# Windowed attention with a gated output: the first four query tiles take their exponentials with the queries on the partitions

## The chip, the cores and the metric

The kernel runs on one core of one Trainium2 chip. The metric is the time of one execution on the device in microseconds (us), as the median of several runs. A profile is one such execution with the hardware profiler on. Its page and its trace name the engines: PE is TensorE's matmuls and PEld its weight loads, DVE is VectorE, ACT is ScalarE, POOL is GpSimd, and SP is the engine whose queue issues nearly all transfers here.

## What is computed

The input x has 8 batches of 1024 tokens with 512 features. In short:

```
xn     = layernorm(x)                          # no weights
q,k,v  = xn @ Wq.T + bq, xn @ Wk.T + bk, xn @ Wv.T + bv     # 16 heads of 32
scores = q @ k.T / sqrt(32), where (i % 256) >= (j % 256), else -1e30
attn   = softmax(scores) @ v
s      = attn @ Wo.T + bo
g      = silu(clip((xn @ sign(fw).T) * scale + bias, -100, 100))
out    = x + s * g                             # all float32
```

A query i sees key j when i modulo 256 is not below j modulo 256. The kernel reorders the tokens so that the four tokens with the same place in a window stand side by side. In that order the mask is block causal: query tile i (128 tokens) sees key tiles 0 to i, and only the tile on the diagonal needs a mask inside it.

## The kernel before

**Tiling.** A batch has 8 token tiles of 128, which form two halves: query tiles 0 to 3 (called f=0) and 4 to 7 (f=1). The 16 heads form 4 groups of 4, and one group fills the 128 partitions of q and k. So there are 32 pairs (b, g) of a batch and a group of heads. Each pair goes through 9 steps, n = 0 to 8, written out in the loop at L1109.

**Two passes over the scores.** Softmax needs a maximum over the keys for each query. The first pass (`maxima_quad`, L501) computes scores with the queries on the partitions into one PSUM tile of four banks, the "quad", one bank for each head, and VectorE reduces it to maxima (`pm`, L537). `shift_parts` (L542) splits the maxima into three bf16 parts, and `shift_rows` (L561) turns these into rows with TensorE. The second pass (`probs_quad`, L586) computes the scores again, now with the keys on the partitions. It first subtracts the maxima by a matmul of the rows with minus ones (L592), then adds the scores (L603) and the mask (L614). ScalarE takes the exponential of all four banks in one instruction (L627), and the result has the layout that `attend_quad` (L633) needs to multiply by v (L640). `S_QUADS` (L43) says which query tiles and key columns are in the first pass's quad of each step, and `T_QUADS` (L56) does so for the second pass.

**Sums.** The denominators are sums over the keys, which lie on the partitions. GpSimd adds up the probability tiles of a half (`add_probs`, L649), and TensorE adds over the partitions with a matmul by ones (`sum_keys`, L678). VectorE inverts the sum in four pieces (`invert`, L713) and multiplies (`normalise_heads`, L717). In the last pair, `sum_quad` (L693) sums each quad on TensorE instead.

**Order of the work.** There is room for one quad alone (`ps_q` has one buffer). The two passes alternate in it: the second pass of pair (b, g) and the first pass of the next pair. While ScalarE or VectorE empties the quad, TensorE does other work: the attend of the step before, and pieces from a list of "beside" work (`Beside.fill`, L953): q and k projections (`q20` is group 2, half 0), values (`V`), gate (`G`, `H`), output (`O`), layernorm turns (`N`). The strings `STEADY`, `OPENING` and `CLOSING` (L804) write that list out by hand for each pair, with a due place for each transfer. Every piece has a cost in us by the program's own count (0.86 for a chunk of four matmuls over 512 columns), and each step is given a share. Engines take their instructions in program order. All transfers but four are issued by SP, in program order too.

**Storage.** Wq and Wk stay transposed in SBUF for the whole run (`wT`, L244). Probability tiles have two buffers (`probs`), the running totals one each for f=0 and f=1.

## Time and profile before

| what | value |
|---|---|
| median of 3 runs | 2209.55 us (2209.39 to 2209.75) |
| the profiled execution's own time | 2209.57 us |
| its span in the trace | 2207.8 us |
| PE busy | 2177.1 us, 99% |
| POOL busy | 1325.8 us, 60% |
| DVE busy | 1276.7 us, 58% |
| ACT busy | 876.8 us, 40% |
| DMA | 93.60 MB, mean 42 GB/s |
| granted TensorE clock | 1.00 in every stretch |
| first and last exponential (L627) start | 79.9 and 2171.7 us |

The span is the time from the first to the last recorded instruction; the rest of the execution's time lies around it. Busy times of PE come from modelled ends of pipelined matmuls, so that neighbours overlap. What a piece of work costs TensorE is better read from a timeline, as the distance from its start to the start of the next piece. The 288 exponentials are 9 for each of 32 pairs.

### The profile page before, as it was taken

Reading aid. Unit: us, or ns where it says so; the run is one execution under the profiler, and the core shown is the slowest. Engines: PE = TensorE matmul, PEld = TensorE weight load, DVE = VectorE, ACT = ScalarE, POOL = GpSimd, SP = SyncE. Lnnn points to the kernel's source line nnn. Section 1 sums busy time; section 2 is a strip of 40 time slices with the busy share of each in tenths; the row PEclk is TensorE's granted clock in tenths of the full one; section 3 lists DMA queues with packets and bytes.
Section 4 is the critical chain, followed back from the end, with each engine's and each line's share of the span. In section 5 each row is a group of like instructions: output and inputs, shape, how many; then the busy total and the mean of one; then the engine's idle time right before and its main releaser. Section 6 shows DMA issues by size and latency. Waiting matters only on the chain. (4 is left out here: it accounts for less than half of the span.)

```text
span 2207.8 us, 57362 instructions
## 1 busy us (share of the span) xinstructions
PE 2177.1 (99%) x26015; PEld 865.2 (39%) x26015; DVE 1276.7 (58%) x1635; ACT 876.8 (40%) x862; POOL 1325.8 (60%) x1198
## 2 busy tenths in 40 slices
PE   8999999999999999999999999999999999999998
PEld 4334433334333443333443333334333443333333
DVE  4556556665557655566555665565655665555564
ACT  2235433444344444344343443434443343333332
POOL 1256566666566656576557765556765666755562
PEclk9999999999999999999999999999999999999999
DMA  4001000121001210012000120002100111000113
GB/s 167 2 16 34 12 7 30 54 73 35 25 25 40 73 35 25 25 57 75 16 25 25 63 68 16 25 26 68 63 16 26 45 58 64 11 21 25 45 54 125
DMA packets 49676, 93.60 MB, mean 42 GB/s; under 512 B 5388, under 2 KB 5656, under 8 KB 49432
## 3 DMA queue, kind: packets, MB, share of 16 engines
q1 hardware_dynamic: 48728, 88.76, 12.1%
q8 instruction: 203, 3.33, 0.6%
q10 hardware_dynamic: 704, 1.18, 0.2%
q14 instruction: 41, 0.34, 0.0%
HBM read 56.37 MB, written 33.55 MB: 41 GB/s over the span
## 5 line engine op out<-in xcount | busy, mean ns | idle before, releaser
L659 POOL TENSOR_TENSOR p<-p,p 128x512 f32<-128x512 f32 x930 | 1096.6, 1209 | 390.0 <-ACT p L627 238.8
L537 DVE TENSOR_REDUCE pm<-s 128x4 f32<-128x2048 f32 (+3 forms) x384 | 664.0, 1750 | 583.6 <-PE s L525 581.7
L627 ACT ACTIVATE p<-t 128x2048 f32<-128x2048 f32 x288 | 540.8, 1878 | 830.7 <-PE t L614 434.7
L715 DVE RECIPROCAL aT<-aT 128x128 f32<-128x128 f32 x256 | 230.3, 928 | 214.6 <-ACT aT L676 214.6
L525 PE MATMUL s<-k,q 32*128 32x512 f32 (+3 forms) x3072 | 315.3, 504 | 1.1 <-ACT q L401 0.8
L640 PE MATMUL av<-p,v 128*32 128x512 f32 (+3 forms) x3072 | 307.4, 495 | 1.6 <-DVE aT L719 1.4
L603 PE MATMUL t<-q,k 32*128 32x512 f32 (+3 forms) x3072 | 301.2, 486 | 0.0
L358 PE MATMUL k_ps<-xnT,wkT 128*32 128x512 f32 (+3 forms) x2832 | 254.9, 477 | 1.7 <-ACT wkT L274 0.7
L358 PE MATMUL q_ps<-xnT,wqT 128*32 128x512 f32 (+2 forms) x2656 | 254.1, 497 | 1.7 <-ACT shift L572 0.8
L358 PE MATMUL v_ps<-wvT,xnT 128*32 128x512 f32 (+3 forms) x2728 | 254.8, 489 | 0.0
L358 PE MATMUL o_ps<-woT,aT 128*32 128x320 f32 (+2 forms) x2568 | 243.9, 503 | 1.5 <-ACT shift L572 0.8
L741 POOL TENSOR_TENSOR s<-s,xb 128x512 f32<-128x512 f32 x63 | 86.2, 1369 | 211.8 <-DVE s L740 209.7
L603 PEld LDWEIGHTS t<-q,k 32*128 32x128 f32 x3072 | 145.1, 185 | 23.4
L358 PEld LDWEIGHTS k_ps<-xnT,wkT 128*32 128x32 f32 x2832 | 83.7, 110 | 169.0 <-issue 138.3
L358 PEld LDWEIGHTS q_ps<-xnT,wqT 128*32 128x32 f32 x2656 | 79.0, 110 | 174.0 <-issue 151.3
L358 PEld LDWEIGHTS v_ps<-wvT,xnT 128*32 128x32 f32 x2728 | 79.2, 109 | 168.6 <-issue 143.4
L525 PEld LDWEIGHTS s<-k,q 32*128 32x128 f32 x3072 | 117.0, 185 | 52.0 <-ACT p L627 42.2
L456 PE MATMUL y_ps<-fwT,x 128*128 128x512 f32 x464 | 135.4, 418 | 1.7 <-ACT k L401 1.3
L640 PEld LDWEIGHTS av<-p,v 128*32 128x32 f32 x3072 | 70.3, 108 | 169.4 <-issue 134.7
L358 PEld LDWEIGHTS o_ps<-woT,aT 128*32 128x32 f32 x2568 | 76.1, 110 | 151.4 <-issue 133.1
L429 POOL TENSOR_TENSOR x<-xnT,x 128x512 fp32r<-128x512 f32 x58 | 74.2, 1279 | 99.9 <-ACT x L428 99.9
L435 POOL TENSOR_SCALAR y<-y 128x512 f32<-128x512 f32 x64 | 39.6, 618 | 152.9 <-DVE y L434 101.1
(96 smaller groups left out, 1478.1 us busy)
## 6 DMA issues: line engine op xcount, KB each, us to landing
g<-t SPq DMA_DIRECT2D x64, 256.0 KB, 2.0
gb<-g SPq DMA_DIRECT2D x64, 256.0 KB, 2.8
xb<-in_L_attn_x_dram SPq DMA_DIRECT2D x64, 256.0 KB, 3.1
out_dram<-s SPq DMA_DIRECT2D x63, 256.0 KB, 2.5
x<-in_L_attn_x_dram SPq DMA_DIRECT2D x62, 256.0 KB, 3.1
wq_st<-in_L_attn_Wq_dram SPq DMA_DIRECT2D x2, 512.0 KB, 5.1
wv_st<-in_L_attn_Wv_dram SPq DMA_DIRECT2D x2, 512.0 KB
fw_st<-in_L_ffn_weights_dram SPq DMA_DIRECT2D x2, 512.0 KB, 9.5
```

What stands on the lines that cost most here:

```text
L358: nc.tensor.matmul(hold[0][cols, lo:hi], lhsT=lhsT[:, cols], rhs=rhs[:, lo:hi], start=(i == 0 and lo == 0), stop=(i == n - 1), skip_group_ ...
L429: nc.gpsimd.tensor_tensor(part[1], src, part[0].bitcast(F32), ALU.subtract)
L435: nc.gpsimd.tensor_scalar(y[0], y[0], MAX_VAL, -MAX_VAL, ALU.min, ALU.max)
L456: nc.tensor.matmul(hold[0], lhsT=part[i][:, c, :], rhs=wT["fw"][:, c, :], start=(i == 0 and c == 0), stop=(i == 1 and c == NC - 1),)
L525: nc.tensor.matmul(sc[:, h, at : at + w], lhsT=qt[b, g][head_rows(h), i * P : (i + 1) * P], rhs=kt[b, g][head_rows(h), lo:hi], start=(at = ...
L537: nc.vector.tensor_reduce(pm[:, 0 if lo == 0 else 1, i, :], sc[:, :, at : at + w], AX.X, ALU.max)
L603: nc.tensor.matmul(sc[:, h, at : at + w], lhsT=kt[b, g][head_rows(h), j * P : (j + 1) * P], rhs=qt[b, g][head_rows(h), q0 : q0 + w], start ...
L627: nc.scalar.activation(pt[:, :, :width], sc[:, :, :width], AF.Exp, scale=SCALE)
L640: nc.tensor.matmul(av[b, g, f][head_rows(h), lo : lo + w], lhsT=vt[b, j][:, g * P + h * DK : g * P + (h + 1) * DK], rhs=pts[b, g, n][:, h, ...
L659: nc.gpsimd.tensor_tensor(t[:, hs, lo : lo + w], t[:, hs, lo : lo + w], p[:, hs, at : at + w], ALU.add)
L715: nc.vector.reciprocal(r, r)
L741: nc.gpsimd.tensor_tensor(s, s, xr, ALU.add)
```

## The change

The eight query tiles are now treated in two ways.

- **Tiles 0 to 3** ("direct"): the first pass's quad is exponentiated where it stands, with queries on the partitions. VectorE's reductions of these tiles run for two heads at a time and give the negated maxima (`nm`). ScalarE takes the exponential for each tile and head with that as a bias, and collects the sum along the row (`own_probs`). VectorE inverts the sums, and GpSimd multiplies the probabilities by them (`own_scale`). VectorE turns every 32x32 block (`own_turn`), and 16 transfers from SBUF to SBUF, each of 32 partitions, put the blocks where a full transpose has them (`move`). `own_attend` multiplies by v. There is no second pass, no row of maxima, no total and no sum by TensorE for these tiles.
- **Tiles 4 to 7** keep the second pass. Their quads are 7 in place of 9.

The steps 0, 3 and 6 hold direct quads, and the steps 0 and 3 have no quad of the second pass. Turns are issued at the head of steps 1, 4 and 8, the moves four at a time at each call of `fill`, and the attends come in steps 4, 7 and the next pair's 1. To make room in SBUF, the transposed Wq and Wk are written to DRAM once and fetched by group (two transfers of 256 KB for each pair). 1/sqrt(32) goes into q. The beside lists, the shares of the steps and the due places of the transfers are written anew. In the last pair the outputs of tiles 0 to 3 (`P`) are beside work, where all eight came after it. The core of the diff:

```diff
 S_QUADS = [
+    [(3, 0, 512)],
+    [(7, 0, 512)],
+    [(6, 0, 512)],
+    [(2, 0, 384), (0, 0, 128)],
     [(4, 0, 512)],
     [(5, 0, 512)],
-    [(6, 0, 512)],
-    [(7, 0, 512)],
+    [(1, 0, 256), (5, 512, 768)],
     [(7, 512, 1024)],
-    [(4, 512, 640), (6, 512, 896)],
-    [(5, 512, 768), (1, 0, 256)],
-    [(3, 0, 512)],
-    [(0, 0, 128), (2, 0, 384)],
+    [(6, 512, 896), (4, 512, 640)],
 ]
...
 T_QUADS = [
-    [(1, 0, 0)],
-    [(1, 1, 0)],
-    [(1, 2, 0)],
-    [(1, 3, 0)],
-    [(1, 4, 0)],
-    [(1, 5, 128), (1, 7, 384)],
-    [(1, 6, 256), (0, 2, 256)],
-    [(0, 0, 0)],
-    [(0, 1, 128), (0, 3, 384)],
+    [],
+    [(0, 0)],
+    [(1, 0)],
+    [],
+    [(2, 0)],
+    [(3, 0)],
+    [(6, 256)],
+    [(5, 128), (7, 384)],
+    [(4, 0)],
 ]
 NQ = len(T_QUADS)
 assert NQ == len(S_QUADS)
-FIRST = {1: 0, 0: 6}
-LAST = {1: 6, 0: 8}
-TOTAL = {1: 0, 0: 7}
+FIRST, LAST = 1, 8
+DIRECT = {0: 4, 3: 4, 6: 2}
...
+    swapped = pool("swapped", 1)
...
+    def keep_weight(name):
+        wd[name] = kept_w.tile([NC, P, NC, P], F32, tag=name, name=f"{name}_d")
+        for c in range(NC):
+            nc.sync.dma_start(
+                wd[name].rearrange("g p c e -> c p g e")[c],
+                wT[name][c].rearrange("p (g e) -> p g e", g=NC),
+            )
+
+    def fetch_slice(name, b, g):
+        t = slices.tile([P, NC, P], F32, tag=name, name=f"{name}_{b}_{g}")
+        nc.sync.dma_start(t, wd[name][g])
+        wslice[name, b, g] = t
...
-                bias=bias[:, g : g + 1], scale=1.0,
+                bias=bias[:, g : g + 1], scale=SCALE if which == "q" else 1.0,
...
+        own = [seg for seg in placed(n) if seg[0] < 4]
+        if own:
+            nm = small.tile([P, 2, NH], F32, tag="nm", name=f"nm_{b}_{g}_{n}", bufs=2)
+            direct[b, g, n] = {"sc": sc, "nm": nm, "own": own}
+            for h in range(0, NH, 2):
+                for k, (i, lo, hi, at) in enumerate(own):
+                    nc.vector.tensor_reduce(
+                        nm[:, k, h : h + 2], sc[:, h : h + 2, at : at + hi - lo],
+                        AX.X, ALU.max, negate=True,
+                    )
+        for i, lo, hi, at in placed(n):
+            if i >= 4:
+                nc.vector.tensor_reduce(
+                    pm[:, 0 if lo == 0 else 1, i - 4, :], sc[:, :, at : at + hi - lo],
+                    AX.X, ALU.max,
+                )
+    def own_probs(b, g, n):
+        it = direct[b, g, n]
+        it["p"] = probs.tile([P, NH, HALF], F32, tag="p", name=f"pd_{b}_{g}_{n}").rearrange(
+            "p h t -> p (h t)"
+        )
+        ls = it["sum"] = small.tile([P, 2, NH], F32, tag="ls", name=f"ls_{b}_{g}_{n}", bufs=2)
+        view = by_slot(it["p"], n)
+        for h in range(NH):
+            for k, (i, lo, hi, at) in enumerate(it["own"]):
+                nc.scalar.activation(
+                    view[:, h, at // P : (at + hi - lo) // P],
+                    it["sc"][:, h, at : at + hi - lo].rearrange(
+                        "p (k r t) -> p k r t", r=NH, t=MT
+                    ),
+                    AF.Exp, bias=it["nm"][:, k, h : h + 1], scale=1.0,
+                    accum_out=ls[:, k, h : h + 1],
+                )
+
+    def own_scale(b, g, n):
+        it = direct[b, g, n]
+        view = by_slot(it["p"], n)
+        used = it["sum"][:, 0 : len(it["own"]), :]
+        nc.vector.reciprocal(used, used)
+        for h in range(NH):
+            for k, (i, lo, hi, at) in enumerate(it["own"]):
+                part = view[:, h, at // P : (at + hi - lo) // P]
+                nc.gpsimd.tensor_scalar(part, part, it["sum"][:, k, h : h + 1], None, ALU.mult)
+    def own_turn(b, g, n):
+        it = direct[b, g, n]
+        size = NH * DIRECT[n] * P
+        t = swapped.tile([P, NH * HALF], F32, tag="pt", name=f"pt_{b}_{g}_{n}")
+        move_some(len(moves))
+        nc.vector.transpose(t[:, 0:size], it["p"][:, 0:size])
+        block = size // NH
+
+        def move(q, r):
+            if "x" not in it:
+                it["x"] = swapped.tile([P, NH * HALF], F32, tag="px", name=f"px_{b}_{g}_{n}")
+            nc.sync.dma_start(
+                it["x"][r * MT : (r + 1) * MT, q * block : (q + 1) * block],
+                t[q * MT : (q + 1) * MT, r * block : (r + 1) * block],
             )
+
+        moves.extend(lambda q=q, r=r: move(q, r) for r in range(NH) for q in range(NH))
...
+    def own_attend(b, g, n):
+        it = direct.pop((b, g, n))
+        k = DIRECT[n]
+        x = it["x"][:, 0 : NH * k * P].rearrange("p (q h k t) -> p h k q t", q=NH, h=NH, k=k, t=MT)
+        first = (b, g, 0) not in av
+        if first:
+            av[b, g, 0] = ps_a.tile([P, HALF], F32, tag="av", name=f"av_{b}_{g}_0")
+        for i, lo, hi, at in it["own"]:
+            for j in range(lo // P, hi // P):
+                for h in range(NH):
+                    nc.tensor.matmul(
+                        av[b, g, 0][head_rows(h), i * P : (i + 1) * P].rearrange(
+                            "p (q t) -> p q t", t=MT
+                        ),
+                        lhsT=vt[b, j][:, g * P + h * DK : g * P + (h + 1) * DK],
+                        rhs=x[:, h, at // P + j - lo // P],
+                        start=first,
+                        stop=(j == hi // P - 1),
+                        skip_group_check=True,
+                    )
+                first = False
+        if n == 6:
+            copy_heads(b, g, 0)
...
+            sides[b, g] = Beside(beside(b, g), [1.8, 1.43, 1.86, 0.86, 1.86, 1.86, 1.36, 2.3, 1.86])
...
+            move_some(4)
...
+        if nxt and n in (1, 4, 8):
+            own_turn(*nxt, {1: 0, 4: 3, 8: 6}[n])
+        spent = 0.0
+        if n in (0, 3):
+            if nxt:
+                maxima_quad(*nxt, n)
             if n == 0:
+                shift_rows(b, g)
+            if before:
+                attend_quad(*before)
+            if nxt:
+                own_probs(*nxt, n)
+            if n == 0 and old:
+                copy_heads(*old, 1)
+                spent += fill(1.2, turns=0)
+                sum_keys(*old)
+            spent += fill(share - spent - 1.0 if nxt else share - spent)
+            if nxt:
+                own_scale(*nxt, n)
+        else:
+            probs_quad(b, g, n)
+            if before:
+                attend_quad(*before)
+            if n == 1:
+                own_attend(b, g, 6)
+            elif n in (4, 7) and nxt:
+                own_attend(*nxt, n - 4)
+            if nxt:
+                gap = {1: 1.6, 4: 1.2, 6: 0.2, 7: 0.8}.get(n, 1.2)
+                spent += fill(gap, kept, 0)
+                if spent < gap - 0.5:
+                    spent += fill(gap - spent, kept)
+                maxima_quad(*nxt, n)
+                if n in DIRECT:
+                    own_probs(*nxt, n)
+                if n == NQ - 1:
+                    shift_parts()
+            if n != FIRST:
+                add_probs(b, g, n)
+        if old and n in (2, 3):
+            invert(*old, 2 * n - 4)
+            invert(*old, 2 * n - 3)
+        if old and n == 4:
+            normalise_heads(*old)
...
+        want = share - spent
+        if nxt and n not in (0, 3):
+            want = max(want, 2.45 if len(S_QUADS[n]) > 1 else 2.35)
             turned_now = now.turn_ahead()
             want -= turned_now
             want -= fill(want, turns=0 if turned_now else 1)
             if want > 0.5:
 
                 want -= fill(want, turns=2)
+        else:
+            fill(max(want, 4.2 - 0.86 - spent) if nxt else want)
+        if nxt and n == 6:
+            own_scale(*nxt, n)
```

The shares of the steps come from `Beside`: the beside work of a pair plus the steps' own list, `[1.8, 1.43, 1.86, 0.86, 1.86, 1.86, 1.36, 2.3, 1.86]`, is divided by nine, and each step's own entry is taken off. The list `S_QUADS` of a step goes with the next pair, the list `T_QUADS` with the present one, as before.

## Prediction

> **What bounds the kernel now.** I read the page's busy times first, then the table of waits, then a timeline of one step of a middle batch.
>
> ```profile
> PE 2177.1 (99%) x26015; PEld 865.2 (39%) x26015; DVE 1276.7 (58%) x1635; ACT 876.8 (40%) x862; POOL 1325.8 (60%) x1198
> ```
>
> TensorE is busy 99% of the span, and no other engine is above 60%. Modelled ends can hide gaps, so the waits of its weight loads are the test:
>
> ```profile
> PEld s L525 <- ACT p L627: 42.2, 97, 0.8
> ...
> PEld L592 <- DVE pm L537: 30.4, 67, 1.8
> ```
>
> These are the two waits on the quad: 42.2 and 30.4 us in all. TensorE almost never waits, so removed TensorE work is time won, as long as nothing else becomes late. One step:
>
> ```profile
> 1065.85 0.40 PE L592 MATMUL t<-shift,neg 3*128 3x512 bf16 x4
> ...
> 1066.07 1.03 PE L603 MATMUL t<-q,k 32*128 32x512 f32 x8
> ...
> 1066.93 0.22 PE L614 MATMUL t<-place_of,after 32*128 32x128 bf16 x4
> ...
> 1067.09 1.07 PE L640 MATMUL av<-p,v 128*32 128x256 f32 x16
> 1067.21 1.88 ACT L627 ACTIVATE p<-t 128x2048 f32<-128x2048 f32 x1 [5.50 <-PE t L614]
> ...
> 1067.97 1.04 PE L358 MATMUL o_ps<-woT,aT 128*32 128x512 f32 x8
> ...
> 1068.83 0.41 PE L566 MATMUL mT_ps<-identb,mt 128*32 128x128 bf16 x16
> ...
> 1069.17 0.23 PE L513 MATMUL s<-after,place_of 32*128 32x128 bf16 x4
> ...
> 1069.24 1.08 PE L525 MATMUL s<-k,q 32*128 32x512 f32 x8
> ...
> 1070.40 2.29 DVE L537 TENSOR_REDUCE pm<-s 128x4 f32<-128x2048 f32 x1 [2.12 <-PE s L525]
> ...
> 1073.02 0.40 PE L592 MATMUL t<-shift,neg 3*128 3x384 bf16 x8
> ```
>
> From start to start, a second-pass quad costs TensorE 1.24 us (1065.85 to 1067.09), an attend 0.88, 16 turns of `shift_rows` 0.34. The one quad is a second clock: second pass 1065.85 to the exponential's end at 1069.09, 3.24 us; first pass 1069.17 to the reduction's end at 1072.69, 3.52; hand-over at least 0.05. That is 6.85 us where the step took 7.17. So a second limit lies close behind the first. A pair (9 steps) takes (2171.7 - 79.9) / 287 x 9 = 65.6 us, of which the quad needs about 62.
>
> **TensorE's work removed, per pair.** Second-pass quads of f=0: 1.24 (step 7), 1.36 (step 8, starts 1073.02 to 1074.38), and half of step 6's 1.30 (1058.33 to 1059.63): 3.25. One sum by ones: 0.85 (1075.27 to 1076.12). One `shift_rows`: 0.34. Together 4.44 us, or 142 us for 32 pairs. `own_attend` multiplies the same 1280 columns as before in pieces of 128; attends of 512, of 384+128 and of 256+256 columns all take 0.88 to 0.89, so I count no change. Its blocks of 32 columns in the moving operand are not in the trace: no gain is in sight, since 0.88 is the same for every shape shown, and 0.88 a pair is the most I allow (40% more). I take 0.
>
> **Work added elsewhere, per pair.** ScalarE: 2.5 exponentials of 1.88 go (4.7); 16 come, four each of 512, 384, 256 and 128 columns.
>
> ```profile
> L627 ACT ACTIVATE p<-t 128x2048 f32<-128x2048 f32 x288 | 540.8, 1878 | 830.7 <-PE t L614 434.7 <-PE t L603 354.8 <-POOL p L659 41.2
> ...
> L401 ACT ACTIVATE k<-k_ps,bias_c 128x512 f32<-128x512 f32 x64 | 44.0, 687 | 117.2 <-PE k_ps L358 117.2
> L435 POOL TENSOR_SCALAR y<-y 128x512 f32<-128x512 f32 x64 | 39.6, 618 | 152.9 <-DVE y L434 101.1 <-PE s L525 44.3 <-PE av L640 7.4
> ```
>
> By the slope to a 512-column copy (584 ns), 0.84 ns a column, and 687 for 512 columns with a bias: 0.69, 0.58, 0.47, 0.36, in all 8.4 us. The collected sum is not in the trace: nothing at best, at most another small instruction of 0.17 (`bias_c`, 12 columns) each, 2.7. I take nothing, because neighbours here overlap by 0.09, which would hide half of it. GpSimd: additions of 7.7 go (3 of 1.28, 4 of 0.97); 16 scalings come. L435 and the 0.23 of a 4-column instruction (L299) give 0.62, 0.52, 0.42, 0.33, in all 7.6; like a two-input addition they would be 15. I take 7.6, the one-input row. VectorE: four inversions (0.93), one multiplication (0.68) and one set of shift parts (1.35) go, 5.8; the finer reductions add 0.5, small inversions 0.6. The turns of 2048, 2048 and 1024 columns are not in the trace: a reduction of 2048 takes 2.29, a plain normalisation of 512 from SBUF 0.54; so 2.2 to 2.29 for the long ones, and at worst twice that. I take 2.29, 5.7 in all. All three engines stay under 70%.
>
> [...] No row here shows a turn.
>
> SP: 48 moves of 64 or 32 KB and 2 weight slices are added to 10 transfers. SP's issues here last 0.33 (`g`) to 0.60 us (`out_dram`), so 50 more take 17 to 30 us of a pair; landing takes 2.0 to 3.1 us at 256 KB. A set of 16 is down 7 to 13 us after its turn. From the turn's end to its attend there are some 18 us for the long sets (steps 1 to 4, 4 to 7) and about 12 for the short one (8 to the next 1). Behind a move, `out`, `gb`, `xb`, `x` and `g` wait in SP's queue; in front of it, an `out` that waits for GpSimd can hold it. I count 0.4 a pair for the short set. Slices are due four blocks (some 14 us) ahead of use, against 2.8 us landing: nothing.
>
> [...]
>
> **Where stalls come, per pair**, with the pair at 61.2 us of TensorE work in place of 65.6.
>
> - Step 0 (tile 3). Score matmuls 1.21, first two heads reduced 1.22, hand-over 0.1, four exponentials 2.76, hand-over 0.1: the quad is free after 5.4. TensorE's cover (scores 1.08, rows 0.34, attend 0.88, sum 0.85, beside work 3.6) is 6.8. (Beside work: the lists of four pairs hold 130 by the program's count, 32.5 a pair; with the steps' own 15.2, a ninth is 5.3, less this step's 1.8, times 1.03 for 0.885 measured against 0.86.) No stall from that, but the rows need `shift_parts`, which ends 1.35 after the reductions that free the quad, while the scores take 1.08: 0.3.
> - Step 3 (tiles 2 and 0). 1.23 + 1.34 + 0.1 + 4 x (0.58 + 0.36) + 0.1 = 6.5; cover 1.08 + 0.88 + 4.6 = 6.5. With summing instructions it is 7.9. I take 0.3. Evacuations of other PSUM banks queue behind these eight exponentials on ScalarE.
> - Step 4. The turn stands ahead of this step's reduction in VectorE's queue, and waits for GpSimd's eight scalings, which wait for step 3's sums. From step 3's start: 6.5 + 0.2 + 3.4 + 0.1 + 2.29 = 12.5; the reduction wants to start at 6.5 + 3.25 + 1.21 = 11.0. Overlaps between GpSimd's instructions (some 0.05 each) take off 0.4: 1.1 late. Behind the turn stand also the gate's and the output's evacuations.
> - Step 1, the same: 5.4 + 0.2 + 2.5 + 0.1 + 2.29 = 10.5 against 6.8 + 4.46 = 11.3: none.
> - Step 7: the exponential's buffer is the one that step 6's attend, queued behind the quad, still reads: 0.3.
> - Elsewhere work and quad come out almost equal (6.75 against 6.81 for steps 1, 2, 4 and 5), so pieces of 0.3 to 0.9 us that don't fit cost some 0.05 at each of 14 hand-overs: 0.6. Before, 0.3 us in each step were to spare.
>
> Sum 0.3 + 0.3 + 1.1 + 0.3 + 0.6 and SP's 0.4: 3.0. The gain is 4.44 - 3.0 = 1.44 a pair, 45 us in 31 pairs.
>
> **Both ends.** Last pair: sums on TensorE fall from 9 to 1 (7.0) on top of 3.25, and five units of beside work (17 us) now fill a pair that waited on its quad, about 3 us; the final inversions, some 2 us, are newly exposed. With the 0.34: minus 12 in all. Start: 9 first-pass steps (35.8 to 78) get 3.4 us of values early (given back in the first pair), but direct steps 3, 1 and 4 stall by about 1, 2.5 and 3 with so little beside them: plus 5. The keeping of weights (8 transfers) runs beside this.
>
> Total: 2209.6 (profiled execution, span 2207.8 and 1.8 around it; the median is 2209.55) - 45 - 12 + 5 = **2158 us**.
>
> **Rivals.**
>
> 1. *TensorE's work alone decides.* If only 0.5 us of stall a pair remain (the turn is quick, sums are free), 3.94 x 31 = 122: 2209.6 - 122 - 12 + 5 = 2081. For it: no engine over 70%. Against: the quad's chain by my rows is as long as the work.
> 2. *The chain scores, exponentials, scaling, turn, reduction decides: slower.* Place: VectorE's queue in steps 1 and 4, in order. With summing instructions, two-input price for scalings (3.9 and 5.3) and the turn at 2.29, step 4 is late by 7.9 + 0.2 + 5.3 + 0.1 + 2.29 - 12.4 = 3.4, step 1 by 0.8, step 3's quad by 1.4; with 1.6 for the other terms, 7.2 of stall, 2.8 more than is won: 2209.6 + 87 - 12 + 5 = 2290. Half of that excess gives about 2245. It decides from 4.7 us of stall a pair (4.44 and 7 / 31). For it: three engines hand one tile on in order. Against: none of the high prices has the nearer row.
> 3. *Moves land late.* SP, blocked by an `out` or at 0.6 an issue, makes the short set 2 us late in each pair in place of 0.4: 2158 + 50 = 2208, no change. For it: SP's waits for GpSimd's `s` come to 470.8 us. Against: most of them pass when nothing is queued.
>
> **How the numbers follow.** Forecast (2105 to 2200) 0.46; rival 1 (below 2105) 0.14; rival 3 and its like (2200 to 2214) 0.10; rival 2 0.30. A measurement can tell 0.2%, 4.4 us: of the 0.10, 0.04 is faster and 0.06 within. So faster 0.64, same 0.06, slower 0.30. The range runs from rival 1 to rival 2's half way, 2081 rounded to 2085, up to 2245; about 0.07 lies below and 0.12 above. Forecast's own range is 2105 to 2200.
>
> **What would show it.** Right: per pair 63 to 65 us between first-pass quads of the same step; TensorE's time at L603, L592, L614 and L681 down by 4.4 us; waits for the quad at step 4 of about 1 us released by VectorE, nearly none at step 0. Wrong: direct exponentials of 512 columns well over 0.69, scalings over 0.62, a turn over 2.3, attends (`own_attend`) that wait for a transfer, or TensorE idle behind evacuations that ScalarE reaches late.

## Result, and the profile after

The kernel before took 2209.65 us (2209.39 to 2212.54), the changed kernel 2740.76 us (2739.90 to 2743.64, 4 runs): a ratio of 1.2402, 95% interval 1.2381 to 1.2424. The forecast was 2158 us, so it had the wrong side and missed by 583 us. The profiled execution has a span of 2739.1 us.

From the page of the changed kernel, the busy times and the granted clock of TensorE:

```profile
PE 2223.4 (81%) x24791; PEld 905.5 (33%) x24791; DVE 1336.3 (49%) x1571; ACT 993.5 (36%) x1824; POOL 1669.7 (61%) x1517
...
PEclk9999999989999998999999999999999999999979
```

TensorE issues 1224 matmuls fewer than before and is busy for longer, because its clock is no longer full everywhere (447 us at half clock by the trace's clock records). Its share falls from 99% to 81%: the span less its busy time was 31 us and is now 516.

The waits of the changed kernel (us in all, times, the longest):

```profile
DVE pt L631 <- POOL pd L622: 413.6, 62, 9.3
...
ACT pd L605 <- DVE nm L579: 268.2, 63, 10.0
...
PE t L728 <- DVE pm L585: 193.7, 52, 7.3
...
ACT pd L605 <- DVE pm L585: 124.9, 32, 4.7
...
PE t L728 <- ACT pd L605: 75.9, 48, 4.6
...
PE av L659 <- DMA px<-pt: 30.2, 9, 4.1
```

Before, the quad cost TensorE 42.2 and 30.4 us. Now it waits 193.7 us for VectorE's reductions (L585) and 75.9 us for the new exponentials (L605) before it may write the next quad. The first line is the chain behind it: VectorE's turns wait 413.6 us for GpSimd's scalings.

Groups of the changed kernel by shape (the columns behind the bar: busy us, mean ns):

```profile
L622 POOL TENSOR_SCALAR pd<-pd,ls 128x512 f32<-128x512 f32 x128 | 198.5, 1567 | 55.4 <-DVE ls L618 55.4
L622 POOL TENSOR_SCALAR pd<-pd,ls 128x384 f32<-128x384 f32 x128 | 159.5, 1246 | 108.4 <-DVE ls L618 108.4
...
L472 POOL TENSOR_SCALAR y<-y 128x512 f32<-128x512 f32 x64 | 44.3, 693 | 219.4 <-DVE y L471 214.7 <-issue 4.8
```

```profile
L605 ACT ACTIVATION_READ_ACCUMULATOR pd<-s,nm 128x1 f32 x512 | 107.8, 210 | 0.0
L605 ACT ACTIVATE pd<-s,nm 128x512 f32<-128x512 f32 x128 | 86.3, 687 | 50.6 <-DVE nm L579 50.6
```

A scaling of 512 columns takes 1567 ns, against the 618 ns of the row that it was priced by (now 693, same line, same columns). An exponential of 512 takes 687 ns, as priced.

One step 3 and 4 in the middle of the changed kernel:

```profile
1366.84 1.06 PE L565 MATMUL s<-k,q 32*128 32x384 f32 x16
...
1368.27 2.42 DVE L579 TENSOR_REDUCE nm<-s 128x2 f32<-128x768 f32 x4
...
1370.80 0.58 ACT L605 ACTIVATE pd<-s,nm 128x384 f32<-128x384 f32 x1 [6.28 <-DVE nm L579]
...
1374.07 0.40 ACT L605 ACTIVATE pd<-s,nm 128x128 f32<-128x128 f32 x1
...
1374.61 0.40 PE L728 MATMUL t<-shift,neg 3*128 3x512 bf16 x4 [0.16 <-ACT pd L605]
...
1374.89 7.24 POOL L622 TENSOR_SCALAR pd<-pd,ls 128x384 f32<-128x384 f32 x8 [0.53 <-DVE ls L618]
...
1377.99 1.14 PE L565 MATMUL s<-k,q 32*128 32x512 f32 x8
...
1382.17 2.31 DVE L631 STREAM_TRANSPOSE pt<-pd 128x2048 f32<-128x2048 f32 x1 [5.74 <-POOL pd L622]
1384.40 2.25 DVE L585 TENSOR_REDUCE pm<-s 128x4 f32<-128x2048 f32 x1
...
1386.71 0.62 PE L728 MATMUL t<-shift,neg 3*128 3x512 bf16 x4 [4.59 <-DVE pm L585]
...
1387.09 1.94 PE L738 MATMUL t<-q,k 32*128 32x512 f32 x8
```

Read it as two holds. **The readers of one quad:** step 3's scores start at 1366.84, the reductions of all four heads run 2.42 us, and only behind the last of them does the first exponential start; the next quad begins at 1374.61, 7.8 us after the scores. **The scaling chain:** eight scalings take 7.24 us, the turn waits for them, and step 4's reduction, whose scores were written by 1379.1, stands behind the turn until 1384.40. TensorE waits 4.59 us. And what follows is slow: eight matmuls that took 1.04 us at 1374.83 take 1.94 here. The clock by stretches of this kernel (columns: us, busy time by engine, granted clock, DMA share, GB/s):

```profile
1386.70:1390.00 3.30, 3.29 (x20) 0.89 (x19) 2.10 (x1) 0.91 (x1) 1.56 (x2) 0.50 0.44 103
...
1393.60:1397.00 3.40, 3.38 (x38) 0.92 (x37) 3.27 (x4) 0.00 (x0) 2.47 (x3) 1.00 0.00 0
```

The granted clock is 0.50 from 1386.1 to 1392.9 by its records and full again after. Over the span the records show 447 us at half clock; in the kernel before the mean is 1.000.

By the starts of the first-pass quads, averaged over the pairs from the sixth to the last but one, a pair of batch and group takes 82.9 us against 66.5 before; TensorE is idle for 15.3 us of it (.34 before) and at half clock for 13.0 (none before). Steps 1 and 4 hold 6.3 of the idle time, steps 0, 3 and 6 hold 7.8. **A sum that recurs:** 66.5, less the 4.44 of work removed, plus idle time above .34, plus half of the time at half clock gives 83.5. It came within about 1 us of the pair's time in each kernel below that keeps the quad in one tile (a3 apart, which adds work); in the three that cut the quad, d2, d3 and e3, it is 1.2 to 1.9 us too low.

### The profile page after: what moved, and what is told of

Its sections match the earlier page's. It is cut to its first block, busy times and chain, and to the rows that moved or that the text cites. A ratio compares the mean times of both kernels' runs of the same rounds, so it can differ in the third digit from the quotient of the medians.

```text
span 2739.1 us, 58797 instructions
## 1 busy us (share of the span) xinstructions
PE 2223.4 (81%) x24791; PEld 905.5 (33%) x24791; DVE 1336.3 (49%) x1571; ACT 993.5 (36%) x1824; POOL 1669.7 (61%) x1517
## 5 line engine op out<-in xcount | busy, mean ns | idle before, releaser
L789 POOL TENSOR_TENSOR p<-p,p 128x512 f32<-128x512 f32 (+1 forms) x736 | 888.3, 1237 | 292.1 <-ACT p L761 289.3
L585 DVE TENSOR_REDUCE pm<-s 128x4 f32<-128x2048 f32 (+3 forms) x256 | 478.9, 1881 | 496.4 <-PE s L565 495.5
L622 POOL TENSOR_SCALAR pd<-pd,ls 128x384 f32<-128x384 f32 (+3 forms) x512 | 546.9, 1087 | 222.6 <-DVE ls L618 222.6
L761 ACT ACTIVATE p<-t 128x2048 f32<-128x2048 f32 (+1 forms) x224 | 393.9, 1758 | 758.8 <-PE t L738 502.0
L605 ACT ACTIVATE pd<-s,nm 128x384 f32<-128x384 f32 (+3 forms) x512 | 262.8, 533 | 401.3 <-DVE nm L579 268.2
L631 DVE STREAM_TRANSPOSE pt<-pd 128x2048 f32<-128x2048 f32 (+1 forms) x96 | 187.6, 1954 | 427.3 <-POOL pd L622 413.6
L728 PE MATMUL t<-shift,neg 3*128 3x512 bf16 (+3 forms) x1024 | 94.7, 377 | 273.4 <-DVE pm L585 193.7
L395 PE MATMUL o_ps<-woT,aT 128*32 128x512 f32 (+3 forms) x2608 | 259.1, 519 | 26.5 <-ACT q L438 12.7
L395 PE MATMUL k_ps<-xnT,wk 128*32 128x512 f32 (+2 forms) x2536 | 252.1, 518 | 18.3 <-DVE y L471 15.9
L395 PE MATMUL q_ps<-xnT,wq 128*32 128x512 f32 (+3 forms) x2704 | 254.7, 498 | 3.0 <-ACT sums L807 1.0
L579 DVE TENSOR_REDUCE nm<-s 128x2 f32<-128x1024 f32 (+3 forms) x256 | 194.9, 814 | 108.9 <-PE s L565 108.2
L472 POOL TENSOR_SCALAR y<-y 128x512 f32<-128x512 f32 x64 | 44.3, 693 | 219.4 <-DVE y L471 214.7
L466 POOL TENSOR_TENSOR x<-xnT,x 128x512 fp32r<-128x512 f32 x59 | 75.7, 1283 | 122.0 <-ACT x L465 122.0
```

Of the source, the lines that this page charges most:

```text
L395: nc.tensor.matmul(hold[0][cols, lo:hi], lhsT=lhsT[:, cols], rhs=rhs[:, lo:hi], start=(i == 0 and lo == 0), stop=(i == n - 1), skip_group_ ...
L579: nc.vector.tensor_reduce(nm[:, k, h : h + 2], sc[:, h : h + 2, at : at + hi - lo], AX.X, ALU.max, negate=True,)
L585: nc.vector.tensor_reduce(pm[:, 0 if lo == 0 else 1, i - 4, :], sc[:, :, at : at + hi - lo], AX.X, ALU.max,)
L605: nc.scalar.activation(view[:, h, at // P : (at + hi - lo) // P], it["sc"][:, h, at : at + hi - lo].rearrange("p (k r t) -> p k r t", r=NH ...
L622: nc.gpsimd.tensor_scalar(part, part, it["sum"][:, k, h : h + 1], None, ALU.mult)
L631: nc.vector.transpose(t[:, 0:size], it["p"][:, 0:size])
```

## Experiments

Times are medians, ratios are to the kernel before on the same chip. Theory A: the scaling chain of steps 1 and 4 is the loss. Theory B: exponentials that start late, and hold the quad or the queue behind them. Theory C: the evacuations of PSUM behind these exponentials (in the texts of a1 and a2 the letter C stands for something else, moves that land late).

**a1, no scaling.** The probabilities of tiles 0 to 3 stay unscaled.

```
-                nc.gpsimd.tensor_scalar(part, part, it["sum"][:, k, h : h + 1], None, ALU.mult)
```

> Left out: GpSimd's multiplication of the direct tiles' probabilities by the inverse sums (L622), so tiles 0 to 3 come out unnormalised; all else stays. Theory A (the turn waits for GpSimd's scalings at the head of VectorE's queue, the reduction behind it comes late, TensorE idles for over 2 us and then runs at a granted clock of 0.5): the idle time of steps 1 and 4 goes (2.0 and 4.3 us a pair) and with it most of the half clock (13.0 us a pair), 10 to 12 us a pair, so 2350 to 2420 us in place of 2741. Theory B (the late exponentials with their accumulator reads, and the evacuations behind them on ScalarE, are the main loss): steps 0, 3 and 6 keep their idle time and the time stays above 2600. Theory C (moves land late): no change beyond 2%.

2438.45 us, ratio 1.1032 (1.1016 to 1.1049): 302 of the 531 us lost are gone, a little less than theory A alone asked for. Idle time falls from 6.3 us per pair to 0.04 in steps 1 and 4, and stays at 7.9 in steps 0, 3 and 6. So there are two causes.

**a2, turn behind the reduction.** VectorE's turn is issued after the reduction of the same step, not ahead of it.

```
-        if nxt and n in (1, 4, 8):
-            own_turn(*nxt, {1: 0, 4: 3, 8: 6}[n])
...
                 maxima_quad(*nxt, n)
+                if n in (1, 4, 8):
+                    own_turn(*nxt, {1: 0, 4: 3, 8: 6}[n])
```

> The whole computation; the turn is issued behind the first-pass quad's reductions in steps 1, 4 and 8, in place of ahead of the second-pass quad. Theory A, if it is the place in VectorE's queue: the reductions of steps 1 and 4 no longer wait for GpSimd, most of their idle time (6.3 us a pair) and half clock goes, 2400 to 2500 us, though the exponential of step 5 may now wait for the turn that frees its buffer. Theory B: above 2600. Theory C: later turns make moves land later, so slower than 2741.

2767.07 us, ratio 1.252 (1.250 to 1.254): theory A's 2400 to 2500 us are missed, and what this text calls theory C came. The reductions are no longer blocked, but the turn comes later, and so do its transfers. From the waits of a2:

```profile
PE av L659 <- DMA px<-pt: 132.6, 33, 6.8
...
PE t L728 <- DVE pm L585: 59.6, 24, 5.0
```

TensorE's wait for reductions falls from 193.7 to 59.6 us, that for moves rises from 30.2 to 132.6. The order in VectorE's queue only chooses who waits for the slow scaling.

**a3, TensorE kept running.** Idle turns (10 to 26 of 128x128) ahead of the second-pass quads of steps 1, 2, 4 and 5, to keep the clock up.

```
+            if nxt and n in (1, 2, 4, 5):
+                warm = bank(f"warm_{b}_{g}_{n}")
+                for _ in range({1: 10, 2: 14, 4: 10, 5: 26}[n]):
+                    nc.tensor.transpose(warm[:, 0:P], ident, ident)
```

> The whole computation, with 10, 14, 10 and 26 idle 128x128 turns on TensorE ahead of the second-pass quads of steps 1, 2, 4 and 5, where it idles. This measures the clock alone: if the granted clock of 0.5 follows from TensorE's idle time and costs what it seems to (13.0 us a pair at half speed, so up to 6.5 us of work), the clock rises to 0.97 or more and the time falls by 100 to 190 us, to 2550 to 2640. If the clock is only a mark of idle time and costs nothing, or does not follow from it: 2741 or more, since the turns add 60 x 0.17 us of work a pair where there is no idle time to take them.

2822.11 us, ratio 1.2761 (1.2741 to 1.2782), half clock down only from 13.0 to 9.5 us per pair. Inconclusive: the turns waited for free banks themselves and did not cover the gaps (TensorE waited at them 44.6 and 24.3 us for evacuations by VectorE).

**a4, the scaling on VectorE.** One multiplication per tile in place of GpSimd's four.

```
+            by = it["sum"][:, k, :].unsqueeze(1).unsqueeze(3).to_broadcast([P, NH, NH, w])
+            nc.vector.tensor_tensor(part, part, by, ALU.mult)
```

> The whole computation; the scalings are one VectorE multiplication for each tile (by the sums spread over the columns) in place of 4 instructions of GpSimd for each tile. Theory A: scaling takes some 2.3 us in place of 6 to 7 for the long sets, so the reductions of steps 1 and 4 are 4 us less late; 2400 to 2480 us. Theory B: above 2600. If VectorE's load is what binds (49% busy, plus some 5.7 us of 83 a pair), slower than 2741.

2490.73 us, ratio 1.1266 (1.1247 to 1.1285). It computes all and is 250 us faster than the changed kernel, 52 slower than a1. Its multiplication of 2048 columns (2478 ns) takes the place of four scalings of 512 (6.3 us).

**b4, forms of the scaling.** Step 0 on contiguous columns, step 3 by a constant (1.5, so these tiles are scaled wrongly), step 6 as it was.

```
+                if n == 0:
+                    part = it["p"][:, h * HALF : (h + 1) * HALF]
+                if n == 3:
+                    by = 1.5
```

> The changed kernel with GpSimd's scalings in three forms; its output is not scaled rightly. Step 0 multiplies contiguous columns by the pointer scalar (it was 16 stretches of 32 columns), step 3 keeps the stretches but multiplies by a constant, step 6 is unchanged. Measured in the changed kernel: 1567 ns for 512 columns, 1246 for 384, 926 for 256, 610 for 128, which is 2.5 ns a column and 290 ns of start. If the stretches are what makes it dear (theory 1), step 0 takes .6 to .8 us per 512 columns; if the pointer scalar is (theory 2), step 3's parts of 384 take about .5 us; if the operation itself runs at this pace on GpSimd (theory 3), all forms stay within 10%, and the total stays within 1% of the changed kernel's 2740 us.

One run, 2677.67 us: 2.3% below the changed kernel, not within 1%. Its groups:

```profile
L627 POOL TENSOR_SCALAR pd<-pd,ls 128x512 f32<-128x512 f32 x128 | 198.2, 1565 | 57.1 <-DVE ls L618 57.1
L627 POOL TENSOR_SCALAR pd<-pd 128x384 f32<-128x384 f32 x128 | 149.9, 1171 | 52.8 <-ACT pd L605 52.7
...
L627 POOL TENSOR_SCALAR pd<-pd 128x128 f32<-128x128 f32 x128 | 67.6, 528 | 0.0
```

Contiguous columns change nothing (1565 against 1567). A constant saves 75 to 82 ns each. So neither the stretches nor the pointer makes it dear, and theory 3 is left. But L472, one operand in and a clamp by two constants, takes 693 for 512 columns. What of it is the multiplication and what the data wasn't tried. A clash with VectorE it is not: in the changed kernel 117 of the 128 scalings of 512 columns run while VectorE stands idle, and take 1564 ns on average.

**b1, exponentials by two heads.** On a4: the exponentials of two heads are issued right behind these heads' reductions.

```
                         AX.X, ALU.max, negate=True,
                     )
+                own_exp(b, g, n, h)
```

> The kernel of a4 (one VectorE multiplication per tile in place of GpSimd's scalings), with one thing moved: the exponentials of the first two heads are issued right behind these heads' two reductions, not behind all four, so that ScalarE need not wait for the maxima of the last two heads. In a4 TensorE stands idle 10.3 us per pair of batch and group, 3.2 of it in step 0, 2.8 in step 3, 1.9 in step 6. Theory B (these three gaps are the quad of scores held too long, because the exponentials begin only after the last of the reductions, about 2.4 us after the first): the exponentials begin about 1.2 us earlier in steps 0, 3 and 6, so the three gaps shrink by about 1 us each, and with the half clock that follows a gap the pair loses 3 to 5 us: 2330 to 2390 us. Theory C (the gaps are TensorE's wait for a free bank, since the evacuations of PSUM stand behind four to eight exponentials in ScalarE's queue): the exponentials end with the last two heads' reductions in front of them as before, the evacuations come little earlier: 2450 to 2500 us.

2606.7 us, ratio 1.1787 (1.1766 to 1.1808): missed, 116 us slower than a4. The second reduction now waits for the first exponentials, and in step 0 the rows' copy came behind the exponentials in this version, so that the sums waited for it, 87.5 us in all. It did not make what it was to make.

**b2, evacuations on VectorE.** On a4: in steps 0 and 3 VectorE makes the evacuations that ScalarE made behind its exponentials.

```
-            nc.scalar.copy(vt[b, it], ps)
+            (nc.vector.tensor_copy if on_vector[0] else nc.scalar.copy)(vt[b, it], ps)
...
                 own_probs(*nxt, n)
+                on_vector[0] = True
```

> The kernel of a4 again, with one thing moved: the evacuations of PSUM that ScalarE makes in steps 0 and 3 behind its exponentials (projections, value rows, the sums, attended heads) are given to VectorE in these two steps. Theory C (they wait behind the exponentials, and TensorE waits for their banks): the gaps of step 0 (3.2 us per pair in a4) and step 3 (2.8) shrink to less than half, and the pair loses 3 to 6 us with the half clock behind them: 2300 to 2400 us. Theory B (the quad of scores is held until the exponentials are through): the gaps stay, and VectorE's added work comes in front of the next reductions: 2470 to 2550 us.

2451.49 us, ratio 1.109 (1.1065 to 1.1114), 39 us less than a4 and short of what theory C expected: idle time in steps 0 and 3 falls from 6.0 to 4.4 us per pair.

**c2, no scaling, both moves** (a1 with b1 and b2).

> The kernel of a1 (GpSimd's scalings left out, so the first four query tiles are not divided by their sums) with both moves together: exponentials issued by two heads, evacuations of steps 0 and 3 on VectorE. It asks what would be left if neither the scaling nor the queue of ScalarE stood in the way. In a1 a pair takes 73.5 us, with TensorE idle for 9.1 and at half clock for 4.9; with an idle of the kernel before, .3, the work alone would be about 62 us, 2060 us in all. Theories B and C together: the idle of steps 0, 3 and 6 (7.9 us per pair) falls under 4, the half clock with it: 2200 to 2290 us. If a third cause holds these gaps (the moves, or the quads of the transposed half waiting for their own exponentials), the idle stays above 6: 2340 us or more.

2556.16 us, ratio 1.156 (1.1541 to 1.158), 118 slower than a1: b1's fault again.

**c3, two tiles for the maxima.** On b1, with the maxima in two tiles and the rows' copy ahead of the exponentials.

```
-            nm = small.tile([P, 2, NH], F32, tag="nm", name=f"nm_{b}_{g}_{n}", bufs=2)
+            nm = [
+                small.tile([P, 2, 2], F32, tag=f"nm{u}", name=f"nm{u}_{b}_{g}_{n}", bufs=2)
+                for u in range(2)
+            ]
```

> The kernel of a4 with the exponentials issued by two heads as in b1, but with what b1 got wrong mended: the negated maxima of heads 0 and 1 and of heads 2 and 3 lie in two tiles of their own. In b1 they shared one tile, and the second reduction waited for the first exponentials to have read it (VectorE's wait for ScalarE at the reductions of L579: 154.6 us, 96 times), while in the changed kernel the first exponential waits for the last reduction, at the same tile. The rows of the maximum's parts are also copied ahead of step 0's exponentials again, as in the changed kernel. Theory B (the gaps of TensorE in steps 0, 3 and 6, in a4 3.2, 2.8 and 1.9 us per pair, are quads of scores held until late exponentials are through): the exponentials now begin with the first reduction and end about 1.2 us earlier, each gap shrinks by about 1 us, and with the half clock behind them the pair loses 3 to 5 us: 2330 to 2400 us. Against it: if ScalarE's own work is what fills these steps, an earlier start only moves its idle time, and the time stays between 2450 and 2500 us.

2530.09 us, ratio 1.1454 (1.1425 to 1.1483): missed, 39 slower than a4.

**c4, c3 with the evacuations on VectorE.**

> The kernel of c3 with the evacuations of steps 0 and 3 on VectorE too, as in b2, which alone took a4 from 2490.7 to 2451.5 us. If the two causes are separate, the gains add: 40 us less than c3. If they are the same gap seen from two sides (the evacuations were late because the exponentials were), less than 15 us.

2515.03 us, ratio 1.1384 (1.1367 to 1.1402): 15 less than c3.

**c5, c4 without scaling.**

> The kernel of c4 with no scaling of the probabilities at all (the first four query tiles are not divided by their sums): what is left of the change when the scaling, the late exponentials and the evacuations behind them are all out of the way. By the sum that has held in every run (66.5 us of the kernel before, less 4.4 of TensorE's work, plus TensorE's idle time above .3 and half of its time at half clock), a pair is under that of the kernel before only if idle time and half of the half clock's time stay under 4.8 us together. In a1 they are 9.1 and 2.4. I expect 6 and 1.2: about 69 us a pair, 2260 to 2330 us, slower than the kernel before even so. Under 2209 us the structure pays and only these three things stood in its way; over 2380 us another cause holds the gaps.

2447.53 us, ratio 1.1083 (1.1066 to 1.1099): missed, and not below a1. A step 0 of c5 says why:

```profile
1322.11 0.69 DVE L591 TENSOR_REDUCE nm<-s 128x2 f32<-128x512 f32 x1 [2.53 <-PE s L572]
1322.91 0.47 ACT L627 ACTIVATE pd<-s,nm 128x256 f32<-128x256 f32 x1 [2.15 <-DVE nm L591]
...
1323.74 0.20 ACT L627 ACTIVATION_READ_ACCUMULATOR pd<-s,nm 128x1 f32 x1
1323.97 0.69 DVE L591 TENSOR_REDUCE nm<-s 128x2 f32<-128x512 f32 x1 [1.17 <-ACT pd L627]
1324.69 0.48 ACT L627 ACTIVATE pd<-s,nm 128x256 f32<-128x256 f32 x1 [0.76 <-DVE nm L591]
```

The second reduction reads other heads, other banks, and writes another tile, and still starts only when the first two heads' exponentials have ended (1323.94). The quad is one tile, and its readers on two engines are put in program order. The chain was only cut differently, and each alternation adds a hand-over (.03 to .11 us in the lines above). Theory B had not been tried yet.

**d1, no maxima.** On a1: the own exponentials subtract a constant, and their reductions are left out.

```
-                    nc.vector.tensor_reduce(
-                        nm[:, k, h : h + 2], sc[:, h : h + 2, at : at + hi - lo],
-                        AX.X, ALU.max, negate=True,
-                    )
...
+    nc.gpsimd.memset(fixed, -8.0)
```

> The kernel of a1 (no scaling) with the maxima of the first four query tiles left out too: their exponentials subtract a constant, so ScalarE can start on the quad of scores as soon as TensorE has written it, and VectorE's reductions of L579 are gone (2.4 us in steps 0 and 3, 1.3 in step 6). In c3 and c5 the reductions and the exponentials of one quad still took turns, with their maxima in separate tiles (VectorE's wait for ScalarE at L579: 154.7 us, 96 times, as in b1): the quad is one tile, and its readers are put in order whatever part of it they read. So theory B has not been tried yet. Theory B: a quad is held by the sum of its reductions and its exponentials (7.8 us in step 3 of the changed kernel), and this sum makes TensorE's gaps of 3.2, 2.8 and 1.9 us in a1; without the reductions the gaps go to about 1 us each, and the pair to 67 us: 2200 to 2300 us. Against it (the gaps are of ScalarE's queue alone): the exponentials begin earlier, but the time falls only by what they came late behind the evacuations, to 2380 to 2440 us.

2243.54 us, ratio 1.0152 (1.0135 to 1.0169): 195 less than a1, as theory B asked. Idle time in step 3 falls from 2.8 to .3 us per pair, in step 6 from 1.9 to 1.0, in step 0 from 3.2 to 2.4; half clock from 4.9 to 1.2.

**d2, the quad in two tiles.** On c3: two tiles of two heads in the same four banks.

```
-        return ps_q.tile([P, NH, 512], F32, tag="quad", name=name)
+        return [
+            ps_q.tile([P, 2, 512], F32, tag=f"quad{u}", name=f"{name}_{u}") for u in range(2)
+        ]
```

> The kernel of c3 (all is computed) with the quad of scores cut into two tiles of two heads each, in the same four banks. Reductions of heads 2 and 3 can now run beside the exponentials of heads 0 and 1, and the next scores of heads 0 and 1 can be written while heads 2 and 3 are still read. It costs one more instruction for each exponential and each reduction of four heads, about .15 us each. Theory B: the quad's chain in steps 0, 3 and 6 is shorter by 1 to 2.4 us, the gaps of 3.4, 3.2 and 2.2 us in c3 shrink to about half, the half clock with them: 2330 to 2430 us against c3's 2530. If the chain is not what holds TensorE: 2500 us or more.

2393.16 us, ratio 1.083 (1.0813 to 1.0846): 137 less than c3. In its timeline the readers overlap, both reductions in a row and the exponentials beside the second:

```profile
1308.60 2.36 DVE L589 TENSOR_REDUCE nm<-s 128x2 f32<-128x1024 f32 x2
...
1309.94 0.69 ACT L626 ACTIVATE pd<-s,nm 128x512 f32<-128x512 f32 x1 [0.16 <-DVE nm L589]
```

**d3, d2 with the evacuations on VectorE.**

> The kernel of d2 with the evacuations of steps 0 and 3 on VectorE (as in b2, which gained 39 us on a4, and in c4, which gained 15 on c3). If with shorter chains the gaps that are left are TensorE's wait for free banks, it gains 40 us or more on d2; if the chain was all, less than 15 us or nothing. It is also the candidate for a version that computes everything: by the sum that has held so far it comes under the kernel before only if idle time and half of the half clock's time stay under 4.8 us a pair, which I do not expect; 2300 to 2420 us.

2404.72 us, ratio 1.0885 (1.0869 to 1.0901): slower than d2. Theory C was worth 39, 15 and minus 12 us: a gain that hangs on the rest of the kernel, and not shown to be a cause of its own.

**e1, scaling kept, no maxima.** The changed kernel with d1's edit. A softmax doesn't depend on the constant, but nothing bounds its exponentials any more.

> The changed kernel with GpSimd's scaling kept and only the maxima of the first four query tiles left out (their exponentials subtract a constant). With the changed kernel (2740 us), a1 (scaling out, 2438) and d1 (both out, 2244) it closes the square: taking the maxima out gained 195 us once the scaling was gone. If the two chains are separate stalls in separate steps (the quad's readers in steps 0, 3, 6; the scaling, turn and reduction in steps 1 and 4), it gains about the same here: 2530 to 2570 us. If the scaling simply moves the stall (it starts 2.4 us earlier here, ahead of the turn), more: under 2500 us. If the scaling's chain covers the other, the gain is under 100 us: 2640 us or more.

2590.15 us, ratio 1.1717 (1.1699 to 1.1735). Taking the maxima out gains 151 us with the scaling and 195 without; taking the scaling out gains 302 with the maxima and 347 without. The gain fell between the bands: the holds add up but for 44 us. Steps 1 and 4 keep their idle time (7.7 us per pair).

**e2, a control:** the kernel before with d2's two tiles.

> A control: the kernel before (nothing of the change) with its quad of scores cut into the two tiles of d2. It pays one more exponential and one more reduction for each quad of four heads, about .15 us each on ScalarE and VectorE. If the readers' turns hold TensorE only where the change has put reductions and exponentials on the same quad (one reader per quad in the kernel before, gaps of .34 us per pair), the time stays within 1% of 2209.6 us, on either side. If cutting the quad in itself shortens every hold, it falls by more than 1%, and part of d2's gain of 137 us on c3 is not due to the change's chain.

2213.28 us, ratio 1.0013 (1.0004 to 1.0022). Cutting the quad gains nothing by itself; what d2 won, it won from the change's chain.

**e3, d2 without scaling.**

> The kernel of d2 with the scaling left out (the first four query tiles are not divided by their sums): a bound for any version that scales elsewhere at no cost. d2 takes 2393 us with 7.2 us of idle per pair, .7 of it in step 4 and 2.0 in step 3. d1, without scaling and without the maxima, takes 2244. If VectorE's multiplication of d2 costs what it does in a4 against a1 (52 us), 2330 to 2350 us; and in no case under the kernel before.

2354.81 us, ratio 1.0649 (1.0631 to 1.0666), 38 below d2 and just above the range.

**f1, no moves.** On d1: the products with v read the turned blocks in place, with two buffers in turn, so these tiles are weighted wrongly.

```
-            nc.sync.dma_start(
-                it["x"][r * MT : (r + 1) * MT, q * block : (q + 1) * block],
-                t[q * MT : (q + 1) * MT, r * block : (r + 1) * block],
-            )
...
+        it["x"] = t
```

> The kernel of d1 (no scaling, no maxima for the first four query tiles) with the SBUF transfers left out as well: the products with v read the turned blocks where VectorE put them, so these tiles are weighted wrongly; all engine instructions stay. In d1 TensorE waits 41.9 us for the moves (17 waits at the products with v of these tiles) and the turns 81 us for the buffer that the moves read (27 waits). If these waits are on the path, the time falls by about 42 us to 2195 to 2210 us, at the level of the kernel before; if the moves stand behind other gaps anyway, it stays at 2235 to 2250 us.

2186.61 us, ratio .9888 (.9872 to .9905): 57 less than d1, where about 42 were expected. The turns' wait for the buffer goes with the moves, and so does their place in SP's queue; these shares were not tried apart. From the pages of d1 and of f1:

```profile
PE 2061.6 (92%) x24791; PEld 857.8 (38%) x24791; DVE 1134.2 (51%) x1315; ACT 991.3 (44%) x1824; POOL 1138.4 (51%) x1006
```

```profile
PE 2048.1 (94%) x24791; PEld 852.3 (39%) x24791; DVE 1129.0 (52%) x1315; ACT 989.9 (45%) x1824; POOL 1139.8 (52%) x1006
```

TensorE's busy time is below the 2177.1 of the kernel before as soon as the scaling is gone (2120.4 in a1). Only with all three gone does the removed work show in the time, and even then 3.5 us of idle time per pair eat most of the 3.9 that a pair saves.

From the changed kernel down: scaling 302, maxima 195, moves 57, in all 554 us, of which 531 bring it back to the kernel before. In another order the first two are 347 and 151. No version that computes all came near: d2 is the best, 8.3% behind.

## Why the prediction was wrong

The sum of stalls was 3.0 us per pair; idle time and half of the half clock's time, less the .34 of before, came to 21.5. The 18.5 over, times 31 pairs, would be 573 of the 583 us. The trace splits the miss a little otherwise: the first pairs lose less than this average, and the two ends add 35 us (last point of the list).

- *TensorE's work removed, 4.44 per pair.* Nearly right. Without idle time and half clock a pair took 66.1 us before and 62.25 in f1: 3.9. The finer products with v cost as little as priced (step 4's ones start at 1375.80, the next matmul .90 later).
- *ScalarE's exponentials.* Right: .69, .59, .47 and .38 measured. The sum is read by an instruction of 210 ns of its own, most of it beside its neighbours: four exponentials of 512 with their reads took 2.78 us in a1 against 2.76 priced.
- *GpSimd, "I take 7.6, the one-input row".* **This step failed, and it is the larger part.** The 16 scalings take 17.4 us per pair, above even the end of 15. Eight of step 3 take 7.24 in place of 3.4. The chain itself was rightly drawn: put 7.24 for 3.4 and step 3's hold of 7.8 for 6.5 into step 4's sum, and the turn ends 17.6 us after step 3's start; in the trace it is 17.8 (1366.73 to 1384.48). Rival 2 had the place, the mechanism and the sign, but its price went no further than 5.3.
- *Step 0, "the quad is free after 5.4", and step 3, "6.5".* **The second step that failed.** Both started the exponentials behind the first two heads' reductions. They start behind all four, since the readers of one quad go in program order: 7.8 in step 3. Here the maxima share one tile too, which would give the same order; but step 6's exponentials wait even for the reduction of the other query tile (L585, 124.9 us), with which they have nothing but the quad in common. Step 6 had no term at all. .6 us were counted for steps 0, 3 and 6, 7.8 measured, as idle time alone. d1 (no reductions) and d2 (two tiles, with e2 as its control) show it from two sides.
- *No term for the clock.* A gap was priced at its own length. In the changed kernel 15.0 us of added idle time brought 13.0 at half clock, 6.5 more.
- *The turn, 2.29.* Right: 2.31 (1.24 for the short one).
- *Moves, .4.* Under-sized: 57 us in d1, 1.8 a pair. No run tried whether the size of the moves is the reason. In the changed kernel SP issues one every 0.63 us, and each lands after 2.0 (64 KB) or 1.9 (32 KB); TensorE's own wait for the moves is 30.2 us in all; they matter once the other holds are gone.
- *The cover of step 0, 6.8.* Beside work is only cover while banks come free, and ScalarE frees them behind its exponentials. Freeing them on VectorE was worth 39 us in a4, less elsewhere.
- *Start and last pair, plus 5 and minus 12.* Both ends were off, and the last pair had the wrong sign. The first-pass quad with which the second pair begins starts at 105.4 us in place of 81.8, 23.6 later; from the last first-pass quad to the end it is 74.3 us in place of 69.8, 4.5 more. In f1 the start is level (81.8) and the end still 4.7 longer; why the last pair gains nothing was not looked into.

Three of the signs set down as "wrong" came: scalings over .62 (1.57), attends that wait for transfers (30.2 us), and TensorE idle behind late evacuations (15.0 us at the values for ScalarE's copy of the sums, L807). Of the signs of "right", a pair of 63 to 65 us and a wait of about 1 us at step 4 did not come (82.9, and 4.59 in the step shown). That the forecast lay far outside was not one price's doing: with the scaling at no cost (a1) the change is still 10% slower.

## What to carry to other kernels

When a change puts a new serial chain between two uses of the one buffer that paces the busiest engine, price every link at the nearest row and again at twice the dearest: here one instruction took 2.5 times its nearest row, and leaving it out was worth 302 us. Ask of each shared tile who else reads it, in which order, and whether that order is by region or by tile; cutting the tile is cheap (e2: 0.13%) and shows it. A version with one cost left out is the quickest way to learn that a kernel has two stalls, and that fixing one is not enough.

## Not expected of the hardware

- **The clock falls after short gaps.** In the changed kernel 86 of 88 stretches at clock 0.5 last 3.41 or 6.83 us. In the step shown TensorE stands idle from 1382.1, the clock halves at 1386.12, .6 us before the quad starts, and comes back 6.83 us later. By the clock records of this trace the starts of all 88 stretches lie on one grid of 3413.3 ns, to within 1 ns. TensorE need not have been idle all through the 3413 ns before a stretch: for the 87 that begin while there is still work, matmuls filled 0 to 49% of that time (by their modelled ends), and the emptiest interval of the grid that was followed by full clock was filled to 41%. The same records show how a stretch ends. In the 45 stretches of one interval that interval is filled to 95% or more; in the 41 of two the first is filled to 8 to 89% (83% in the step shown, whose first .6 us are idle) and the second to 97% or more.
- **GpSimd multiplies one operand by a scalar slower than it adds two:** 1567 ns against 1283 for 512 columns in the same kernel (L622 above, and L789):

```profile
L789 POOL TENSOR_TENSOR p<-p,p 128x512 f32<-128x512 f32 x608 | 761.8, 1283 | 280.8 <-ACT p L761 278.0
...
L815 DVE TENSOR_TENSOR aT<-aT,sums 128x512 f32<-128x512 f32 x31 | 38.5, 1242 | 0.0
```

- **VectorE's multiplication of two SBUF operands** (L815, 512 columns) takes 1242 ns here on average, where the kernel before took 681 with one operand in PSUM (L719); in the step shown it runs 2.23 us, beside GpSimd's two-operand instructions. The trace says that the two take turns: in 25 of the 31 calls GpSimd is ahead, and what is left of the multiplication's time without the overlap is .54 to .55 us; in five others the multiplication is ahead and takes .67 to .68, and the addition issued right behind it takes 1.74 to 1.78 us in place of 1.28. No run tried it apart.
